# A third state tile, rows nine apart in HBM and filler matmuls in a four-layer network with a selective scan

## The chip, the cores and the metric

One core of one Trainium2 chip runs the whole program. The metric is the device time of one execution in microseconds (us). The kernel before takes 15384.8 us, the median of 3 runs (15377.52 to 15408.42).

## The reference, cut to what matters

The input x is (16, 192, 32, 32). Four layers follow each other, each in the form x = x + layer(group_norm(x)). Layer 0 is an mLSTM block with convolutions, layer 1 a channel attention with depthwise convolutions, layer 3 a roll-and-weight block with a 1x1 convolution. The change lies in layer 2, a selective scan over the 1024 pixels of an image in four directions (by rows, by columns, and both reversed), for 384 channels with 16 states each:

```python
D_INNER = 384
K = 4
N = 16
R = 12
...
        def step(h, xs_t):
            d_t, u_t, B_t, C_t = xs_t
            dA = jnp.exp(d_t[..., None] * A)
            h = h * dA + (d_t * u_t)[..., None] * B_t[:, :, None, :]
            y = jnp.einsum('bkdn,bkn->bkd', h, C_t)
            return (h, y)
...
    x_dbl = jnp.einsum('bkdl,kcd->bkcl', xs, x_proj_w)
    dts, Bs_, Cs_ = jnp.split(x_dbl, [R, R + N], axis=2)
    dts = jnp.einsum('bkrl,kdr->bkdl', dts, dt_w)
    delta = jax.nn.softplus(dts + dt_b[None, :, :, None])
    A = -jnp.exp(A_logs).reshape(K, D_INNER, N)
    ys = selective_scan(xs, delta, A, Bs_, Cs_, Ds.reshape(K, D_INNER))
```

## The kernel before, in words

**Stages.** `layer0` (L153) runs alone for about the first 3.1 ms. Then `LayersB` (L843) does layers 1 to 3: `prepare` (L1150) is layer 1 and the head of layer 2 of one image, `scans` (L1636) the scans of an image, `complete` (L1376) the end of layer 2 and layer 3. While the scans of image b run, `prepare` of image b+1 and `complete` of image b-1 are woven in between them as two background streams.

**The scans.** A unit of work is 16 channels with 8 states each, laid out as 128 partitions of 1024 pixels. Two units (`BLOCKS`) make a group of 16 channels with all 16 states, 24 groups a direction, 4 directions an image: 192 units, called slots, an image, and 3072 in all. For unit u of group n:

- `load_group` (L1811) loads the rows of delta (`dl`) and delta times u (`du`) of 16 channels from the HBM tensors `dld` and `dud`, each row repeated on 8 partitions: 16 rows of 4 KB read 8 times, 512 KB. `load_states` (L1807) loads the B and C rows (`bb`, `cb`) from `xdr` in the same way, 8 rows repeated 16 times, once a direction. The tiles `dl` and `du` have two buffers each.
- `decay` (L1851, ScalarE) makes dA = exp(dl times A); it is issued two slots ahead (`AHEAD`). `inputs_up` (L1845, ScalarE) copies `du` into one of two PSUM tiles `xt`, one group ahead.
- `inputs` (L1857, VectorE) multiplies `xt` by `bb`, both blocks of a group at the head of an even slot. `scan` (L1862, VectorE) then runs h = dA times h + xt along the pixels into `h[u % 2]`: two tiles of states, so that scan u can't start before the reader of scan u-2 is done.
- `outputs` (L1871, GpSimd) multiplies h by C into `hc`, one slot after the scan. `sums` (L1891, TensorE) adds the states up with a 0/1 matrix, four 32-row matmuls, one more slot later. `collect` (L1916, ScalarE) moves the accumulator out every fourth unit.

**The step sizes.** `front` (L1746) gives the pieces that make B, C, delta and delta times u of the next directions, at fixed slots of the 48 of a direction, counted from the direction's start (-24, -22, -18, -12, -6, 0, 6, 12 and a few after each). `ends` writes |x| into the tile `e` and relu(x) into `dlh`; `logs` turns `e` into log(1 + exp(-|x|)) in place; `park` adds `e` to `dlh` and multiplies by x into `duh`, both on GpSimd, and stores `dlh` and `duh` to HBM (L1794, L1795). Their matmuls use the PSUM bank "bf"; the two streams use "bp" and "bc".

**What sets the order.** The schedule is written by the program itself, with no reordering later (`manual_schedule`). `scans` keeps an estimated clock for each engine. A slot has an estimated length (`SLOT` = 4.83 us for an even one, 2.31 us for an odd one). In each slot it issues, in this order: inputs and scan, `outputs`, `sums`, `inputs_up`, `decay`, `collect`, the loads (`fetch`, L1820), the `front` pieces that are due, and then as many background pieces as the estimates (`Metered`, L782, `fits`, L1705) say will fit. An engine runs its instructions in that order, so a late instruction holds all that stands behind it. All loads and stores shown above are issued by SyncE's queue, in order as well. Near the end of an image, at slot 161 (`FETCH`), the head of the next image is completed and `fetch_xx` (L1372) loads its 1.5 MB `xx`, which `front` reads from slot 168 on, in the place of the current one.

Every operation of the background streams has the line L800 in the profile, since a helper (`Metered.issue`) records it.

Of the kernel before, what the change touches and what calls it, by code (L numbers as in the profile page):

```python
# [11 lines left out]
F32 = mybir.dt.float32  # L12
# [7 lines left out]
C, H, W = 192, 32, 32  # L20
L = H * W
# [752 lines left out]
ENGINES = ("PE", "ACT", "POOL", "DVE")  # L774
ALLOW = {"PE": 2.45, "DVE": 0.3}
OVER = {"PE": (0.8, 1.2), "ACT": (0.0, 1.5), "POOL": (0.5, 1.5)}
LEAST = {"PE": 1.0, "ACT": 0.6, "POOL": 0.8}
TABLE = 1.28
MARGIN = 0.6


# [61 lines left out]
class LayersB:  # L843
# [81 lines left out]
    def setup(self):  # L925

        tc, nc, cx, wp, I, NB = self.tc, self.nc, self.cx, self.wp, self.I, self.NB
        dp = self.dp
        self.dqd = dp.tile([6, 128, 9, 128], F32, name="dqd")
        self.dvd = dp.tile([2, 2, P6, 9, P6], F32, name="dvd")  # L930
        self.vd = dp.tile([P6, 2, L], F32, name="vd")
        self.x0d = dp.tile([P6, 2, L], F32, name="x0d")
        self.x2d = dp.tile([P6, 2, L], F32, name="x2d")
        self.xdr = dp.tile([K, 2 * N, L], F32, name="xdr")
        self.dld = dp.tile([K, 3, 128, L], F32, name="dld")
        self.dud = dp.tile([K, 3, 128, L], F32, name="dud")
        self.xxd = dp.tile([3, 128, L], F32, name="xxd")
        self.yd = dp.tile([3, 128, L], F32, name="yd")
        self.zd = dp.tile([NB, 3, 128, L], F32, name="zd")
        self.x1d = dp.tile([NB, P6, 2, L], F32, name="x1d")  # L940


        bn_g, bn_b = self.vec("bn_g", P6), self.vec("bn_b", P6)
        self.bsc = wp.tile([P6, 2], F32, name="bsc")
        self.bsh = wp.tile([P6, 2], F32, name="bsh")
        with tc.tile_pool(name="b_pre0", bufs=1) as pre:
            st = pre.tile([P6, 2, NB, 12], F32, name="st")
            for a in range(2):
                nc.scalar.dma_start(
                    st[:, a], self.sdram[:, a * P6 : (a + 1) * P6, :].rearrange("b p s -> p b s")  # L950
                )
            mv = pre.tile([P6, 2, 2], F32, name="mv")
            for a in range(2):
                nc.vector.bn_aggr(mv[:, a, :], st[:, a].rearrange("p b s -> p (b s)"))
            sd = pre.tile([P6, 2], F32, name="sd")
            nc.scalar.activation(sd, mv[:, :, 1], AF.Sqrt, bias=cx.eps5[0:P6])
            nc.vector.reciprocal(sd, sd)
            nc.vector.tensor_mul(self.bsc, sd, bn_g)
            nc.vector.tensor_mul(sd, mv[:, :, 0], self.bsc)
            nc.vector.tensor_sub(self.bsh, bn_b, sd)  # L960


        self.offb = wp.tile([P6, P6], F32, name="offb")
        nc.sync.dma_start(self.offb, I["c_off48"])
        self.temp = wp.tile([P6, 2], F32, name="temp")
        for a in range(2):
            for j in range(2):
                nc.sync.dma_start(
                    self.temp[48 * j : 48 * j + 48, a : a + 1],
                    I["temperature"][2 * a + j : 2 * a + j + 1].unsqueeze(0).to_broadcast([48, 1]),  # L970
                )

        self.dw2b = self.vec("dw_b", 128)
        self.pads = [wp.tile([128, H + 2, W + 2], F32, name="pad%d" % i) for i in range(2)]
        for t in self.pads:
            nc.gpsimd.memset(t, 0.0)

        self.xx = wp.tile([128, 3, L], F32, name="xx")
    def setup_scans(self):
# [52 lines left out]

        ring = lambda name, n, shape: [wp.tile(shape, F32, name=name + str(i)) for i in range(n)]
        self.y = wp.tile([128, 3, L], F32, name="y")
        self.dA, self.h, self.hc = ring("dA", 3, [128, L]), ring("h", 2, [128, L]), ring("hc", 3, [128, L])
        self.dl, self.du = ring("dl", 2, [128, L]), ring("du", 2, [128, L])
        self.bb, self.cb = ring("bb", BLOCKS, [128, L]), ring("cb", 3, [128, L])
        self.e, self.dlh, self.duh = (wp.tile([128, HL], F32, name=n) for n in ("e", "dlh", "duh"))
        self.xd = wp.tile([64 + XR, L], F32, name="xd")
        self.dtw = wp.tile([64 + R, INNER], F32, name="dtw")  # L1040
        self.xt = [self.xp.tile([128, L], F32, name="xt%d" % i) for i in range(2)]
# [108 lines left out]
    def prepare(self, b):  # L1150
# [67 lines left out]

        id6 = cx.ident[0:P6, 0:P6]
        at = sm.tile([P6, 2, P6], F32, tag="at", name="at", bufs=1)  # L1220
        kk = sm.tile([P6, 2, C], F32, tag="m1", name="kk", bufs=1)[:, :, 0:P6]
        rq = sm.tile([P6, 2], F32, tag="rq", name="rq")
        vs = [self.p4([P6, 2, HL], "vh") for _ in range(2)]
        for hf in range(2):
# [19 lines left out]
        for a in range(2):  # L1244
# [5 lines left out]
                nc, pk[:, ch(a)], [(qT[:, t, k0 : k0 + P6], qT[:, t, k0 : k0 + P6]) for t in range(NCH)]  # L1250
            )
        yield "DVE", 0
        nc.vector.tensor_mul(
            kk, pk.rearrange("p (a c) -> p a c", a=2), id6.unsqueeze(1).to_broadcast([P6, 2, P6])
        )
# [34 lines left out]
        yield "ACT", 0  # L1290
        for a in range(2):
            nc.scalar.mul(at[:, a, :], at[:, a, :], den[:, a : a + 1])
        m1 = sm.tile([P6, 2, C], F32, tag="m1", name="m1", bufs=1)
        m2 = sm.tile([P6, 2, C], F32, tag="m2", name="m2", bufs=1)
        for m_, w_ in ((m1, w1), (m2, wpf)):
            yield "PE", 0
            p = self.mm()[0:P6, 0 : 2 * C]
            for a in range(2):
                nc.tensor.matmul(p[:, a * C : (a + 1) * C], lhsT=at[:, a, :], rhs=w_[:, a, :], start=True, stop=True)
            yield "ACT", 0  # L1300
            nc.scalar.copy(m_, p.rearrange("p (a c) -> p a c", a=2))
        ds = [self.taps(P6, self.dvd[1, 0], I["dw_kv"][ch(0)], b == 0)]
        for hf in range(2):
            for a in range(2):
# [331 lines left out]
    def scans(self, b, more, carry):  # L1636
# [9 lines left out]
        for t in range(UNITS):  # L1646
            now = clock["DVE"]
            for e in ENGINES:
                clock[e] = max(clock[e], now)
            for s in (self.before, self.after):  # L1650
                while s.engine == "ACT" and not s.late and self.fits(s, now + SLOT[t % BLOCKS]):
                    self.advance(s)
            if t % BLOCKS == 0:
                for u in range(t, t + BLOCKS):
                    self.inputs(u)
            self.scan(t)
            clock["DVE"] += SLOT[t % BLOCKS]
            end = now + SLOT[t % BLOCKS]
            if t > 0 or carry:
                self.outputs((t - 1) % UNITS, t == 0)  # L1660
                clock["POOL"] += OWN["POOL"]
            if t > 1 or carry:
                self.sums((t - 2) % UNITS)
            if t % BLOCKS == BLOCKS - 1 and (more or t + 1 < UNITS):
                self.inputs_up((t + 1) % UNITS)
                clock["ACT"] += OWN["INPUTS"]
            if more or t + AHEAD < UNITS:
                self.decay((t + AHEAD) % UNITS)
                clock["ACT"] += OWN["DECAY"]
            if t > 1 or carry:  # L1670
                self.collect((t - 2) % UNITS)
            self.fetch(t, more, carry)
            self.bank = "bf"
            was = dict(self.spent)
            for piece in ahead.pop(t, ()):
                piece()
            for e in ENGINES:
                clock[e] += self.spent[e] - was[e]
            for e in ALLOW:
                have[e] = min(have[e], 0.0) + ALLOW[e] - self.spent[e] + was[e]  # L1680
            if more and t == FETCH:
                while self.parked < b + 2:
                    self.advance(self.after)
                self.fetch_xx()
            if t == UNITS - DIR_UNITS:
                while self.read < b:
                    self.advance(self.before)
            if t == 2:
                self.scanned = b
            streams = (self.before, self.after)[:: 1 if t % 2 else -1]  # L1690
            while any(self.fits(s, end) for s in streams):
                for s in streams:
                    if self.fits(s, end):
                        self.advance(s)
            self.slots += 1
        self.turns += K * more
        if not more:
# [4 lines left out]
                self.sums(u)  # L1702
            self.collect(UNITS - 1)

    def fits(self, s, end):  # L1705

        if not s.open(self.slots) or s.engine == "SP":
# [2 lines left out]
        if s.engine != "DVE":  # L1710
            end += OVER[s.engine][self.slots % BLOCKS]
        wait = s.inputs()
        if wait > at and (s.engine == "DVE" or wait + LEAST[s.engine] > end):
            return False
        return at < end + 0.1 and self.have.get(s.engine, 1.0) > 0.0

# [145 lines left out]
    def scan(self, u):  # L1862
        nc = self.nc
        n, blk = divmod(u, BLOCKS)
        k = n // GROUPS
        views = [self.h[u % 2], self.dA[u % 3], self.xt[(n + 1 + blk) % 2]]
        if k >= 2:
            views = [v[:, ::-1] for v in views]
        nc.vector.tensor_tensor_scan(*views, 0.0, op0=ALU.mult, op1=ALU.add)  # L1869

    def outputs(self, u, carried=False):  # L1871
# [1 line left out]
        n, blk = divmod(u, BLOCKS)  # L1873

        k = n // GROUPS - K * (carried and u == UNITS - 1)
        views = [self.hc[u % 3], self.h[u % 2], self.c_of(k, blk)]
        if n // GROUPS % 2:
            views = [views[0].rearrange("p (h w) -> p w h", w=W)] + [
                v.rearrange("p (w h) -> p w h", h=H) for v in views[1:]
# [147 lines left out]
```

## Time and profile before

| quantity | value |
|---|---|
| median of 3 runs | 15384.8 us |
| the profiled execution | 15416.19 us, of which the span from first to last instruction is 15414.4 us |
| busy over the span | PE 80%, DVE 80%, POOL 67%, ACT 59% |
| mean granted TensorE clock | 0.832 |
| scan stage, 3320 to 15250 us | 11930 us: DVE busy 10705.61, PE 9204.12, POOL 9503.52, ACT 7872.19; clock 0.80 |
| scan (DVE, L1869) | x3072, mean 2274 ns |
| input products (DVE, L1860) | x3072, mean 1227 ns |
| outputs (POOL, L1881) | x3072, mean 2371 ns |
| decay (ACT, L1853), copy of du (ACT, L1849) | 1146 ns each of 3072, 1014 ns each of 1536 |

How to read it: PE is TensorE, DVE VectorE, ACT ScalarE, POOL GpSimd, SP SyncE. A row of an engine gives its busy time and the idle time just before its instructions, with what ended that idle time ("<-"). The granted clock is the share of TensorE's full speed that its throttle let through. An fp32 matmul stands in the trace as two MATMUL records.

### The profile page before, as it was taken

How to read it: one execution, taken by the hardware profiler on the slowest of the kernel's cores; microseconds unless marked ns; L12 is line 12 of the kernel's file. 1: busy time of each engine (PE TensorE's matmuls, PEld its weight loads, DVE VectorE, ACT ScalarE, POOL GpSimd, SP SyncE). 2: the span in 40 equal slices, each digit the busy share in tenths (PEclk: the TensorE clock that was granted, in tenths of full speed). 3: DMA queues.
4: the chain of work that ended last, by engine and by line, in shares of the span. 5: the costliest groups of instructions: out<-in, count | busy, mean ns of one | idle time of the engine just before them, and what ended most of it. 6: DMA issues, size and time to landing. Idle time of an engine off the chain costs nothing.

```text
span 15414.4 us, 184312 instructions
## 1 busy us (share of the span) xinstructions
PE 12384.4 (80%) x65856; PEld 4810.3 (31%) x65856; DVE 12329.6 (80%) x10115; ACT 9160.4 (59%) x11881; POOL 10313.5 (67%) x6314
## 2 busy tenths in 40 slices
PE   8999999977777778777778787787878787878755
PEld 4444444422222222222222222222222222222212
DVE  4444444469988988888898989898988888889897
ACT  3333333345666666666666666666666666666665
POOL 2222222237787878787887878787878787878785
PEclk9999999978878887888888888887878787878766
DMA  1000000047878777878777777777777777777774
GB/s 30 15 15 15 17 15 15 14 126 185 214 181 212 185 207 182 208 180 210 189 203 191 199 195 198 195 198 194 197 196 194 195 197 199 194 200 186 200 182 129
DMA packets 884782, 2412.09 MB, mean 156 GB/s; under 512 B 146672, under 2 KB 266944, under 8 KB 876224
## 3 DMA queue, kind: packets, MB, share of 16 engines
q1 hardware_dynamic: 871168, 2397.50, 60.8%
q8 instruction: 532, 8.72, 0.2%
q10 hardware_dynamic: 12736, 3.04, 0.1%
q14 instruction: 346, 2.83, 0.1%
HBM read 2019.10 MB, written 364.30 MB: 155 GB/s over the span
## 4 chain that ended last, share of the span: by engine, by line
PE 19%; DVE 16%; POOL 14%; issue 13%; DMA 10%; ACT 7%; SPq 1%; DVEq 0%; POOLq 0%; ACTq 0%
PE mm L800 15%; DVE h L1869 10%; POOL hc L1881 9%; DVE xt L1860 5%; DMA dl<-dld 3%; PE acc L1911 3%; DMA du<-dud 2%; POOL t L800 2%; ACT dA L1853 2%; ACT xt L1849 2%; DMA y<-ydram 1%; DMA yh<-yd 1%; POOL dlh L800 1%; PE acc L1902 1%; DMA yd<-y 1%
## 5 line engine op out<-in xcount | busy, mean ns | idle before, releaser
L1881 POOL TENSOR_TENSOR hc<-h,cb 128x1024 f32<-128x1024 f32 x3072 | 7245.8, 2371 | 2087.6 <-DVE h L1869 1591.0
L1869 DVE TENSOR_TENSOR_SCAN h<-dA,xt 128x1024 f32<-128x1024 f32 x3072 | 6914.6, 2274 | 299.1 <-POOL hc L1881 292.0
L1860 DVE TENSOR_TENSOR xt<-xt,bb 128x1024 f32<-128x1024 f32 x3072 | 3633.2, 1227 | 904.0 <-ACT xt L1849 771.3
L1853 ACT ACTIVATE dA<-dl,A 128x1024 f32<-128x1024 f32 x3072 | 3507.3, 1146 | 810.3 <-DMA dl<-dld 703.4
L1911 PE MATMUL acc<-hc,sel 128*32 128x256 f32 x24576 | 2406.9, 473 | 1717.2 <-POOL hc L1881 1714.3
L800 PE MATMUL mm<-pad,dg 128*128 128x512 f32 (+1 forms) x5580 | 2911.4, 657 | 13.3 <-ACT pad L800 10.6
L1849 ACT COPY xt<-du 128x1024 f32<-128x1024 f32 x1536 | 1557.8, 1014 | 1350.9 <-DVE h L1869 1163.1
L627 POOL TENSOR_TENSOR D<-D,mask 128x256 f32<-128x256 f32 x768 | 542.7, 738 | 2101.1 <-DVE D L624 2101.1
L1911 PEld LDWEIGHTS acc<-hc,sel 128*32 128x32 f32 x24576 | 561.8, 120 | 4060.2 <-POOL hc L1881 2905.2
L800 PEld LDWEIGHTS mm<-pad,dg 128*128 128x128 f32 (+1 forms) x5580 | 999.1, 193 | 1491.8 <-issue 1370.3
L800 PE MATMUL mm<-x,wgt 96*128 96x512 f32 (+1 forms) x1664 | 1053.7, 769 | 146.8 <-ACT o L800 56.4
L1902 PE MATMUL acc<-y,ident 128*128 128x512 f32 x576 | 442.3, 859 | 447.3 <-ACT y L1921 445.9
L800 POOL TENSOR_TENSOR t<-x 96x768 f32<-96x768 f32 (+4 forms) x510 | 647.3, 1289 | 216.9 <-PE mm L800 216.8
L800 PE MATMUL mm<-d,xT 128*96 128x256 f32 x2048 | 567.9, 415 | 5.4 <-ACT o L800 5.0
L800 POOL TENSOR_TENSOR duh<-dlh,xx 128x512 f32<-128x512 f32 x384 | 537.6, 1400 | 30.1
L800 POOL TENSOR_TENSOR dlh<-dlh,e 128x512 f32<-128x512 f32 x384 | 488.5, 1272 | 103.0 <-ACT e L800 101.0
L800 PEld LDWEIGHTS mm<-x,wgt 96*128 96x128 f32 (+1 forms) x1664 | 339.3, 224 | 672.1 <-issue 363.5
L800 PE MATMUL mm<-xd,dtw 12*128 12x512 f32 x768 | 535.6, 783 | 10.3 <-ACT z L800 10.3
L391 PE MATMUL pc<-ypad,w_c 128*64 128x512 f32 (+1 forms) x1152 | 480.3, 664 | 74.2 <-PEq L751 41.5
L624 DVE SCALAR_TENSOR_TENSOR D<-D,s 128x256 f32<-128x256 f32 x768 | 272.0, 416 | 255.2 <-ACT D L620 255.2
L620 ACT ACTIVATE D<-s 128x256 f32<-128x256 f32 x768 | 233.4, 390 | 338.2 <-PE s L613 332.5
L800 PEld LDWEIGHTS mm<-d,xT 128*96 128x96 f32 x2048 | 328.0, 174 | 261.0 <-issue 164.0
(321 smaller groups left out, 14487.7 us busy)
## 6 DMA issues: line engine op xcount, KB each, us to landing
dl<-dld SPq DMA_DIRECT2D x1536, 512.0 KB
du<-dud SPq DMA_DIRECT2D x1536, 512.0 KB
dld<-dlh SPq DMA_DIRECT2D x384, 256.0 KB
dud<-duh SPq DMA_DIRECT2D x384, 256.0 KB
bb<-xdr SPq DMA_DIRECT2D x128, 512.0 KB
cb<-xdr SPq DMA_DIRECT2D x128, 512.0 KB
dg<-dqd SPq DMA_DIRECT2D x270, 192.0 KB
zd<-z SPq DMA_DIRECT2D x48, 512.0 KB
```

Source lines behind the costliest of these rows:

```text
L391: nc.tensor.matmul(p[r, :], lhsT=w_, rhs=v, start=(n == 0), stop=(n == 14))
L620: nc.scalar.activation(d, S[j][:, two], AF.Exp)
L624: nc.vector.scalar_tensor_tensor(d, d, 2.0, S[j][:, 2 * CH :], op0=ALU.min, op1=ALU.mult)
L627: nc.gpsimd.tensor_mul(d, d, mask)
L800: return f(out, *args, **kw)
L1849: self.nc.scalar.copy(self.xt[n], self.du[n])
L1853: self.nc.scalar.activation(self.dA[u % 3], self.dl[n % 2], AF.Exp, scale=self.A[:, blk, n : n + 1])
L1860: self.nc.vector.tensor_mul(self.xt[(n + 1 + blk) % 2], self.xt[n % 2], self.bb[blk])
L1869: nc.vector.tensor_tensor_scan(*views, 0.0, op0=ALU.mult, op1=ALU.add)
L1881: self.nc.gpsimd.tensor_mul(*views)
L1902: nc.tensor.matmul(acc, lhsT=self.cx.ident, rhs=self.y[:, g, half(pair)], start=True, stop=False)
L1911: nc.tensor.matmul(self.acc[rows4(q), q4(s)], lhsT=self.sel[:, m, :], rhs=self.hc[u % 3][:, q4(q)], start=False, stop=(s + m + blk == 3),)
```

## The change

- `h` becomes a ring of three tiles; `scan` and `outputs` index it with u % 3.
- To make room, the tile `e` is no longer a tile of its own but `duh`; `kk` of `prepare` takes a background slot "pa", and `m1` and `m2` take the two slots "w" of the weights.
- `xdr`, `dld` and `dud` are allocated with a further dimension of 9 (`PITCH`), of which only index 0 is used: a row of 4 KB lies 36 KB from the next one and no longer 4 KB.
- A new method `keep_busy` is called at the end of each slot. If TensorE's estimated clock lies more than 0.4 us (`IDLE`) before the slot's estimated end, it issues n matmuls of 128 by 256 (two MATMUL records each) whose result nobody reads, n being the room divided by 0.46 us (`FILL`), into the bank "bf", from `ident` and the first 256 columns of `xx`. It does nothing in the slots of `FRONT` and the two after each (23 of the 48 slots of a direction), and none in the last four slots of an image.
- `LEAST` becomes pairs with equal members, which changes no value.

```diff
+PITCH = 9
+FRONT = (-24, -22, -18, -12, -6, 0, 6, 12)
+IDLE, FILL = 0.4, 0.46
...
-        self.xdr = dp.tile([K, 2 * N, L], F32, name="xdr")
-        self.dld = dp.tile([K, 3, 128, L], F32, name="dld")
-        self.dud = dp.tile([K, 3, 128, L], F32, name="dud")
+        self.xdr = dp.tile([K, 2 * N, PITCH, L], F32, name="xdr")[:, :, 0, :]
+        self.dld = dp.tile([K, 3, 128, PITCH, L], F32, name="dld")[:, :, :, 0, :]
+        self.dud = dp.tile([K, 3, 128, PITCH, L], F32, name="dud")[:, :, :, 0, :]
...
-        self.dA, self.h, self.hc = ring("dA", 3, [128, L]), ring("h", 2, [128, L]), ring("hc", 3, [128, L])
+        self.dA, self.h, self.hc = ring("dA", 3, [128, L]), ring("h", 3, [128, L]), ring("hc", 3, [128, L])
...
-        self.e, self.dlh, self.duh = (wp.tile([128, HL], F32, name=n) for n in ("e", "dlh", "duh"))
+        self.dlh, self.duh = (wp.tile([128, HL], F32, name=n) for n in ("dlh", "duh"))
+        self.e = self.duh
...
-        kk = sm.tile([P6, 2, C], F32, tag="m1", name="kk", bufs=1)[:, :, 0:P6]
...
+        kk = self.slot("pa", [P6, 2, P6], "kk")
...
-        m1 = sm.tile([P6, 2, C], F32, tag="m1", name="m1", bufs=1)
-        m2 = sm.tile([P6, 2, C], F32, tag="m2", name="m2", bufs=1)
-        for m_, w_ in ((m1, w1), (m2, wpf)):
+        ms = []
+        for w_ in (w1, wpf):
...
+            m_ = self.slot("w", [P6, 2, C], "m", 2)
+            ms.append(m_)
...
+            self.keep_busy(t, end)
             self.slots += 1
...
+    def keep_busy(self, t, end):
+        at = t % DIR_UNITS
+
+        if any(0 <= (at - a) % DIR_UNITS <= 2 for a in FRONT) or t >= UNITS - 4:
+            return
+        n = int((end - self.clock["PE"] - IDLE) / FILL)
+        if n <= 0:
+            return
+        self.bank = "bf"
+        p = self.mm()
+        for i in range(n):
+            self.nc.tensor.matmul(
+                p[:, 0:256], lhsT=self.cx.ident, rhs=self.xx[:, 0, 0:256], start=True, stop=True
+            )
+        self.clock["PE"] += n * FILL
...
-        views = [self.h[u % 2], self.dA[u % 3], self.xt[(n + 1 + blk) % 2]]
+        views = [self.h[u % 3], self.dA[u % 3], self.xt[(n + 1 + blk) % 2]]
...
-        views = [self.hc[u % 3], self.h[u % 2], self.c_of(k, blk)]
+        views = [self.hc[u % 3], self.h[u % 3], self.c_of(k, blk)]
```

More of the change, by code (lines that the diff above doesn't have):

```diff
@@ L776 @@
 OVER = {"PE": (0.8, 1.2), "ACT": (0.0, 1.5), "POOL": (0.5, 1.5)}
-LEAST = {"PE": 1.0, "ACT": 0.6, "POOL": 0.8}
+LEAST = {"PE": (1.0, 1.0), "ACT": (0.6, 0.6), "POOL": (0.8, 0.8)}
 TABLE = 1.28
+PITCH = 9
+FRONT = (-24, -22, -18, -12, -6, 0, 6, 12)
+IDLE, FILL = 0.4, 0.46
 MARGIN = 0.6
@@ L1300, in prepare @@
             yield "ACT", 0
+            m_ = self.slot("w", [P6, 2, C], "m", 2)
+            ms.append(m_)
             nc.scalar.copy(m_, p.rearrange("p (a c) -> p a c", a=2))
+        m1, m2 = ms
         ds = [self.taps(P6, self.dvd[1, 0], I["dw_kv"][ch(0)], b == 0)]
@@ L1712, in fits @@
         wait = s.inputs()
-        if wait > at and (s.engine == "DVE" or wait + LEAST[s.engine] > end):
+        if wait > at and (s.engine == "DVE" or wait + LEAST[s.engine][self.slots % BLOCKS] > end):
             return False
```

## The prediction

> **What bounds the kernel now.** I read first the engines' busy time over the scan stage (the view of stretches, for 3320 to 15250 us; columns are length, then busy time of PE, PEld, DVE, ACT, POOL, then TensorE's clock, DMA share, GB/s).
>
> ```profile
> 3320.00:15250.00 11930.00, 9204.12 (x42460) 3210.49 (x42460) 10705.61 (x7115) 7872.19 (x9492) 9503.52 (x5234) 0.80 0.77 196
> ```
>
> VectorE is busy for 10,706 of 11,930 us, 90%: a floor, since the change takes no work from it. What can be won is its idle time, 11,930 - 10,706 = 1,224 us. So I asked next what VectorE waits for, and what ScalarE waits for, since it comes first there (3300 to 15000 us: total, times, longest).
>
> ```profile
> DVE xt L1860 <- ACT xt L1849: 766.9, 361, 30.0
> DVE h L1869 <- POOL hc L1881: 290.4, 231, 3.4
> DVE yh L800 <- PE mm L800: 40.7, 16, 5.0
> ...
> ACT dA L1853 <- DMA dl<-dld: 684.0, 237, 8.9
> ACT pad L800 <- PE mm L800: 345.9, 137, 6.4
> ACT xg L800 <- PE mm L800: 170.4, 75, 8.3
> ```
>
> The first row says that ScalarE's copy of du is late. It stands in ScalarE's queue behind evictions of the background streams, so I followed each of the 361 waits back to the last idle time of ScalarE before that copy. There it had waited for a TensorE matmul in about 540 us of the 767, for the load of `dl` in 110, for the store `zd` in 49, for `du` in 35. The same walk along GpSimd for the second row ends, for 173 of 297 us (the walk to the span's end counts 297), at `t` waiting for a matmul: its tile is free only when TensorE has read it. So some 750 us of VectorE's idle time begin at TensorE.
>
> The chain of waits over 3400 to 15250 us agrees; PE's shares are the largest:
>
> ```profile
> by line: PE mm L800 17.9%; issue 16.0%; DVE h L1869 12.7%; POOL hc L1881 11.9%; DVE xt L1860 6.2%; DMA dl<-dld 4.0%; PE acc L1911 3.7%; DMA du<-dud 3.1%; POOL t L800 3.1%; ACT dA L1853 2.8%; ACT xt L1849 2.7%; DMA y<-ydram 1.2%; DMA yh<-yd
> ```
>
> Why is TensorE late when it is only 77% busy? Two stretches of the same matmul (timeline: start, us, what):
>
> ```profile
> 8002.33 2.84 PE L800 MATMUL mm<-pad,dg 128*128 128x512 f32 x6
> ...
> 8010.45 3.78 PE L800 MATMUL mm<-pad,dg 128*128 128x512 f32 x4
> ```
>
> 0.47 us a record in one, 0.95 in the other: TensorE runs at full clock or at half. The planner's estimate for such a matmul (0.06 + 0.0017 x 512 = 0.93 us for two records) holds at full clock only.
>
> [...] its clock records hold only 1.0 and 0.5, in multiples of 3413 ns, and 40% of the scan stage is at 0.5 (0.6 x 1 + 0.4 x 0.5 = 0.80). Set beside TensorE's busy share in each window [...] of 591 half-clock windows under 80% busy none was followed by full clock, of 722 over 90% more than half were; of 279 full-clock windows under 40% busy none stayed full, of those over 60% at least 83%.
>
> [...] The trace has this: packets of 4 KB take 279 ns (median of 359 stretches with only `dl` and `du` moving), and 159 ns in the loads of `zd`[...]. In the view of stretches, last columns:
>
> ```profile
> 8028.00:8031.00 3.00, 1.89 (x13) 0.92 (x12) 3.00 (x2) 2.97 (x6) 2.29 (x2) 0.53 1.06 240
> 15268.00:15269.60 1.60, 0.45 (x8) 0.00 (x0) 1.60 (x3) 0.00 (x0) 1.60 (x1) 0.50 0.82 315
> ```
>
> 240 GB/s with all engines busy against 315 at 82%, that is 384.
>
> **The change part by part.**
>
> *Third h tile.* Scan u then waits for the output product of u-3, which has at least one odd slot (2.31 us planned) more; the waits average 290.4/231 = 1.26 us, 3.4 at most. So the 290 us go at that place. What is late next: in the list of VectorE's waits, 128 of these us are followed within 16 us by a wait for ScalarE, whose own cause (TensorE, DMA) isn't moved; there VectorE only arrives earlier and waits longer. 290 - 128 = 162: I take 165, with 60 and 290 as ends.
>
> *Filler matmuls.* Their number: I put each matmul record of the scans into its slot by order (a slot starts with the 8 records of L1911) and priced it as the planner does. The mean is 2.67 us a slot. Odd slots (2.31 us) have hardly any room; the even ones outside the blocked slots take 2.8 to 5.6 fillers, in all at most 2,680, since the planner's clock also counts waits. At full clock one costs two records of half the `pad` matmul's 512 columns, 2 x 0.47/2 = 0.47 us: 2,680 x 0.47 = 1,260 us of TensorE time, at the slot's end, where TensorE mostly waits next for `hc` (1,700 us, L1911 on L1881); that idle time is their cover. At half clock it is twice that and cover is gone in a late slot. The gain: they raise the busy share in 25 of 48 slots; half-clock time is as high in the blocked slots (0.51 to 0.57 in slots 0, 6, 8, and 0.72 in 30), where they do nothing. I estimate half clock falling from 40% to 28% of the stage. Lateness falls faster than that share, as short delays vanish wholly: I take 40% of the 540 + 41 us of waits that begin at TensorE: -230. Ends: -500 (clock near 1) and +0.
>
> *What fillers add by reading `xx`.* `fetch_xx` overwrites `xx`. Its load is issued at slot 162 of an image and lands 11.3 to 12.3 us later (15 images). The slot's own fillers (its planned load is 1.7 us, so about 5) read `xx`, so TensorE stands still until the load lands, about slot 165; behind it stand the sums, both streams' matmuls, then ScalarE's evictions and its copy of du. VectorE has some slack: I take 6 us of the 11.5, x 15 = +90. Ends: 0 and 170. SyncE in turn waits at that load for the fillers of slot 160: past by then, nothing.
>
> *Pitch.* If 4 KB packets fall from 279 to about 170 ns, a 512 KB load (8 packets an engine) falls from 2.2 to 1.4 us. A late `dl` is one that lands 7.7 us after its issue (median of the late ones, against 4.7 for all), as it stands behind other loads; with dl, du and bb some 60% of DMA time, about 2 to 2.5 us of that go, of a mean wait of 684/237 = 2.9. From VectorE's 110 + 35 + 49 and 16 us for `bb`, 210 in all, I take 55%: -115. [...] the ends are -210 and +40[...].
>
> *e in duh, kk, m1 and m2 in slots.* `ends` now also waits for the store of `duh`, issued last, with a landing of 5.5 us (median; 10.4 at the 95th percentile), three slots or some 12 us ahead. For `dlh`, stored one step earlier, the same wait came to 0.5 us in all. I take +10 (0 to 40). The load of `wx` now waits on SyncE for the last matmul with m1, with loads of `dl` queued behind: 15 x up to 3 us, mostly inside the 2 to 3 slots that a load has: +5 (0 to 45).
>
> Sum: -165 - 230 + 90 - 115 + 15 = -405. The profiled execution takes 15,416 us (its span 15,414), 31 over the median; I take the same -405 from the median 15,385: **14,980 us**, 2.6% less.
>
> **The rivals.** *Warm* (15%): TensorE stays at full clock nearly throughout, and `t`, evictions and copies come in time. Then -500 for the fillers, -250 for h, -150 for DMA, +90: -810, 14,575 us. [...] Against: blocked slots. *Moved* (21%): the wait for `hc` turns into one for ScalarE's copy, and the pitch changes nothing: -60 - 150 + 90 = -120, 15,265 us. For it: the two rows of waits stand close; against: 162 us have no such neighbour. *On the path* (9%), the other side: fillers run in slots that are late already, at a mean of both clocks, 0.70 us each: 1,880 us. PE has 2,806 of 11,930 us on the chain, 24%; with that share they cost 450, and with xx 170, 620; less 280 for h and pitch, +340: 15,725 us. Place: the end of even slots, in front of `sums`. It decides once more than 6% of filler time is on the path with no gain in clock ((280 - 170)/1,880), or 18% with the 230 us. Against it: TensorE's largest wait is right there. *Nothing* (4%): gains and stalls cancel.
>
> **How the numbers follow.** Main case 51%, -250 to -600. Warm 15%, Moved 21%, Nothing 4%, On the path 9%. A measurement here tells 0.2% (31 us) from no change. Faster: 51 + 15 + 20 = 86%; same: 4 + 1 = 5%; slower: 9%. The range runs from 14,600 (leaving out most of Warm, about 8%) to 15,300 (leaving out Nothing, On the path and no more).
>
> **What would show it.** DVE h on POOL hc from 290 to under 60 us. The clock in the scan stage from 0.80 to about 0.86, with 4,000 to 5,400 more MATMUL records. Stretches of `dl` and `du` alone at over 320 GB/s and a DMA share near 0.6; the late `dl` from 684 to about 300 us. A TensorE wait of about 9 us for xx<-xxd, 15 times. The forecast is wrong if the clock stays near 0.80, if the packets stay near 279 ns, or if DVE xt on ACT xt grows past 767 us.

## The result and the profile after

The changed kernel takes 15404.58 us (median of 20 runs, 15371.51 to 15420.25), the kernel before 15376.78 us in the same comparison: a ratio of 1.0016 with a 95% interval of 1.001 to 1.0022. It lies outside the range of 14,600 to 15,300 around the forecast of 14,980 us, and the sign was wrong too. The profiled execution's span is 15407.7 us. Lines have moved by 30 in the scans (the scan is now L1899, inputs L1890, decay L1883, copy of du L1879, outputs L1911, sums L1941); the helper of the background streams is L805, the fillers L1730.

The scan stage in the view of stretches (same columns as before: length, busy PE, PEld, DVE, ACT, POOL, clock, DMA share, GB/s):

```profile
3320.00:15250.00 11930.00, 9603.73 (x45310) 3729.36 (x45309) 10682.84 (x7122) 7872.99 (x9497) 9511.30 (x5238) 0.85 0.75 196
```

The clock went from 0.80 to 0.85, close to the forecast of 0.86, but with only 2,850 more MATMUL records (2,836 of them the fillers') where 4,000 to 5,400 were forecast. VectorE's busy time is what it was, so it idles as long as before. Its waits, and ScalarE's (3300 to 15000 us: total, times, longest), show what the idle time is made of now:

```profile
DVE xt L1890 <- ACT xt L1879: 1029.6, 373, 34.2
DVE h L1899 <- POOL hc L1911: 40.5, 39, 2.0
...
ACT dA L1883 <- DMA dl<-dld: 576.2, 209, 8.4
ACT z L805 <- PE mm L805: 361.1, 63, 16.2
ACT pad L805 <- PE mm L805: 275.5, 121, 7.8
```

The wait for `hc` has all but gone (290 to 40 us); the wait for ScalarE's copy of du has grown by as much (767 to 1,030), which the prediction had named as a sign of being wrong. From 3300 us to the end VectorE is idle for 1,331 us before and 1,358 after. The late `dl` fell by 108 us only, and ScalarE's `z` waits 241 us longer for a matmul (before: 119.7). TensorE's own waits give the reason for that last row:

```profile
PE acc L1941 <- POOL hc L1911: 1308.1, 844, 7.5
PE acc L1932 <- ACT y L1951: 267.1, 146, 4.7
PE mm L1730 <- DMA xx<-xxd: 223.8, 15, 15.6
```

The third row did not exist before: 15 times the fillers stand until the new `xx` has landed. The chain of waits (3400 to 15250 us) has it too, as two new members, `PE mm L1730` and `DMA xx<-xxd`, in place of what L805 gave up:

```profile
by line: issue 17.1%; PE mm L805 16.4%; DVE h L1899 13.8%; POOL hc L1911 11.4%; DVE xt L1890 7.3%; DMA dl<-dld 3.9%; PE acc L1941 3.8%; POOL t L805 3.1%; ACT xt L1879 2.5%; ACT dA L1883 2.0%; PE mm L1730 1.9%; DMA xx<-xxd 1.5%; PE acc L1932
```

One of the 15 stalls in the timelines of PE, SP and DVE (start, us, what, idle before it). The load leaves SyncE's queue at 3930.82; the fillers of a slot behind it stand on TensorE for 14.75 us, and VectorE then for 16.15:

```profile
3926.98 0.64 PE L1941 MATMUL acc<-hc,sel 128*32 128x256 f32 x8
3942.37 2.04 PE L1730 MATMUL mm<-xx,ident 128*128 128x256 f32 x4 [14.75 <-DMA xx<-xxd]
```

```profile
3930.82 0.53 SPq L1383 DMA_DIRECT2D xx<-xxd  x1
```

```profile
3937.26 4.45 DVE L1899 TENSOR_TENSOR_SCAN h<-dA,xt 128x1024 f32<-128x1024 f32 x2
3957.86 2.37 DVE L1890 TENSOR_TENSOR xt<-xt,bb 128x1024 f32<-128x1024 f32 x2 [16.15 <-ACT xt L1879]
```

### The profile page after: what moved, and what is told of

Its sections match the earlier page's. It is cut to its first block, busy times and chain, and to the rows that moved or that the text cites. A ratio compares the mean times of both kernels' runs of the same rounds, so it can differ in the third digit from the quotient of the medians.

```text
span 15407.7 us, 189554 instructions
## 1 busy us (share of the span) xinstructions
PE 12783.2 (83%) x68692; PEld 5329.9 (35%) x68692; DVE 12295.1 (80%) x10115; ACT 9156.4 (59%) x11881; POOL 10312.6 (67%) x6314
## 4 chain that ended last, share of the span: by engine, by line
PE 20%; DVE 18%; POOL 14%; issue 13%; DMA 8%; ACT 6%; SPq 1%; DVEq 0%; POOLq 0%; ACTq 0%
PE mm L805 14%; DVE h L1899 11%; POOL hc L1911 9%; DVE xt L1890 6%; DMA dl<-dld 3%; PE acc L1941 3%; POOL t L805 2%; ACT xt L1879 2%; ACT dA L1883 2%; PE mm L1730 1%; DMA xx<-xxd 1%; PE acc L1932 1%; POOL dlh L805 1%; DMA du<-dud 1%; DMA yh<-yd 1%
## 5 line engine op out<-in xcount | busy, mean ns | idle before, releaser
L1911 POOL TENSOR_TENSOR hc<-h,cb 128x1024 f32<-128x1024 f32 x3072 | 7243.1, 2372 | 2065.0 <-DVE h L1899 1456.1
L1899 DVE TENSOR_TENSOR_SCAN h<-dA,xt 128x1024 f32<-128x1024 f32 x3072 | 6889.3, 2270 | 40.5 <-POOL hc L1911 40.5
L1890 DVE TENSOR_TENSOR xt<-xt,bb 128x1024 f32<-128x1024 f32 x3072 | 3632.3, 1227 | 1163.0 <-ACT xt L1879 1033.6
L1883 ACT ACTIVATE dA<-dl,A 128x1024 f32<-128x1024 f32 x3072 | 3505.9, 1146 | 650.8 <-DMA dl<-dld 595.0
L1941 PE MATMUL acc<-hc,sel 128*32 128x256 f32 x24576 | 2241.4, 442 | 1375.9 <-POOL hc L1911 1373.4
L805 PE MATMUL mm<-pad,dg 128*128 128x512 f32 (+1 forms) x5580 | 2909.6, 657 | 13.2 <-ACT pad L805 11.0
L1879 ACT COPY xt<-du 128x1024 f32<-128x1024 f32 x1536 | 1557.3, 1014 | 1275.8 <-DVE h L1899 1094.6
L1941 PEld LDWEIGHTS acc<-hc,sel 128*32 128x32 f32 x24576 | 543.0, 116 | 3495.4 <-POOL hc L1911 2376.8
L805 PEld LDWEIGHTS mm<-pad,dg 128*128 128x128 f32 (+1 forms) x5580 | 995.5, 192 | 1476.1 <-issue 1360.9
L1730 PE MATMUL mm<-xx,ident 128*128 128x256 f32 x2836 | 917.3, 471 | 228.6 <-DMA xx<-xxd 223.8
L805 PE MATMUL mm<-x,wgt 96*128 96x512 f32 (+1 forms) x1664 | 992.5, 729 | 102.5 <-ACT o L805 51.3
L1730 PEld LDWEIGHTS mm<-xx,ident 128*128 128x128 f32 x2836 | 632.9, 236 | 549.3 <-issue 430.3
L805 POOL TENSOR_TENSOR t<-x 96x768 f32<-96x768 f32 (+4 forms) x510 | 647.7, 1291 | 252.4 <-PE mm L805 248.5
L805 POOL TENSOR_TENSOR dlh<-dlh,duh 128x512 f32<-128x512 f32 x384 | 488.6, 1272 | 115.7 <-ACT duh L805 115.7
L805 POOL TENSOR_TENSOR duh<-dlh,xx 128x512 f32<-128x512 f32 x384 | 538.1, 1401 | 30.1
L805 PE MATMUL mm<-d,xT 128*96 128x256 f32 x2048 | 546.9, 403 | 0.5 <-POOL d L805 0.5
L805 PEld LDWEIGHTS mm<-x,wgt 96*128 96x128 f32 (+1 forms) x1664 | 323.3, 213 | 593.1 <-issue 344.8
L805 PE MATMUL mm<-xd,dtw 12*128 12x512 f32 x768 | 491.5, 723 | 4.7 <-ACT z L805 4.7
```

The lines of the kernel that those rows point to most:

```text
L805: return f(out, *args, **kw)
L1730: self.nc.tensor.matmul(p[:, 0:256], lhsT=self.cx.ident, rhs=self.xx[:, 0, 0:256], start=True, stop=True)
L1879: self.nc.scalar.copy(self.xt[n], self.du[n])
L1883: self.nc.scalar.activation(self.dA[u % 3], self.dl[n % 2], AF.Exp, scale=self.A[:, blk, n : n + 1])
L1890: self.nc.vector.tensor_mul(self.xt[(n + 1 + blk) % 2], self.xt[n % 2], self.bb[blk])
L1911: self.nc.gpsimd.tensor_mul(*views)
```

## The experiments

Effects in us below are (ratio - 1) times 15,385, so that each run is taken against its own runs of the kernel before; 0.001 is 15 us. The changed kernel is +25.

### The parts, one at a time

The fillers read a constant tile in place of `xx` (a_perm), or are left out (b_nofill):

```diff
-                p[:, 0:256], lhsT=self.cx.ident, rhs=self.xx[:, 0, 0:256], start=True, stop=True
+                p[:, 0:256], lhsT=self.cx.ident, rhs=self.perm[:, 0:2].rearrange("p j h w -> p (j h w)"), start=True, stop=True
```

> The changed kernel, with the fillers reading a constant tile (perm) in the place of xx; number, shape and place of the fillers stay. Theory A (the fillers' read of xx eats what the rest gains): TensorE's 224 us of waiting for xx<-xxd go, slot 162 to 165 is short again, some 190 us are won: about 15,210 us. Theory B (the fillers delay TensorE's real work in general, xx is only one place of many): 15,330 or more.

> The changed kernel without the fillers (third h tile, aliases and pitch stay). Theory A: the h tile gains part of its 290 us, about 15,250 us, and TensorE's clock is back at 0.80. Theory C (the wait for hc only turns into one for ScalarE's copy of du, whatever the fillers do): 15,360 to 15,390, with DVE xt on ACT xt near 1,000 us.

Measured: a_perm 15313.79 us, ratio 0.9955 (0.9941 to 0.9968), -69; b_nofill 15339.1 us, 0.9973 (0.9963 to 0.9983), -42. So the read of `xx` costs 25 + 69 = 94 us, half of what theory A gave it, and fillers without it bring 69 - 42 = 27, give or take some 25. In a_perm ScalarE's `z` waits 108 us for a matmul, no longer than before the change (120). In b_nofill VectorE waits 933 us for the copy of du, which is nearer to theory C than to A.

The third tile with its aliases alone, without fillers and with rows 4 KB apart (c_h3: `PITCH = 1`, no `keep_busy`), and the pitch alone in the kernel before (d_pitch: the three allocations of the diff):

> Third h tile and the aliases alone: no fillers, rows 4 KB apart. If the pitch is worth nothing, as the unchanged 4 KB packets say (264 ns after, 269 before), this equals the run without fillers within 0.2%. If the pitch helps the late loads of dl, this one is 50 us or more slower than that.

> The kernel before with the rows 36 KB apart and nothing else. Pitch worth nothing: within 0.2% of before (15,377), 4 KB packets at 265 to 270 ns, late dl near 684 us. Pitch of use: 15,300 or less.

Measured: c_h3 15364.02 us, 0.9984 (0.9976 to 0.9993), -25; d_pitch 15362.7 us, 0.9987 (0.998 to 0.9993), -20. Together -45, against -42 for both in b_nofill: these two parts add up, and the whole is -42 - 27 + 94 = +25. The median 4 KB packet takes 265 ns in d_pitch, 269 in the kernel before. VectorE's waits in c_h3 (3300 to 15000 us):

```profile
DVE xt L1889 <- ACT xt L1878: 982.6, 408, 34.0
DVE h L1898 <- POOL hc L1910: 43.2, 38, 2.0
```

The exchange of 247 us of one wait for 216 of the other is thus the doing of the third tile and its aliases, with no filler in the kernel. Averaged by slot over images 1 to 14 it can be followed: slots 96 to 103 of an image become 2.73 us shorter, and slots 104 to 111 give 2.26 of them back. There the waits for `hc` at slots 103, 105 and 107 (8.3 us an image) become a wait for a matmul at 106 (2.5), for `hc` at 108 and 109 (2.7) and for `dl` at 111 (0.5 to 3.2).

The fillers of a_perm in the kernel before (j_fill):

> The kernel before with the fillers alone, reading the constant tile. If the parts add up, 25 us (as between the changed kernel without fillers and with fillers on the constant tile) less than before: 15,350 to 15,365. If fillers and the third h tile need each other: no difference, or more time than before, here.

Measured: 15381.81 us, 1.0002 (0.9994 to 1.0011), with a clock of 0.84 in the scan stage. Alone, in this number and these slots, the fillers bring nothing that can be measured.

### The loads of dl and du

Only the source of the loads changes, so that 128 different rows are read and none twice; the scans get wrong operands. g_distinct does it in c_h3, m_h2dist in the kernel before:

```diff
-                t, src[k, g, i * CW : (i + 1) * CW, :].unsqueeze(1).to_broadcast([CW, NBL, L])
+                t, src[k, g]
```

> The kernel with the third h tile alone (15,364 us), but each load of dl and du takes 128 different rows of the same tensor in the place of 16 rows 8 times each (so the scans work on wrong operands, with the same instructions and bytes). Theory F (reading the same row over and over is what slows the packets, and distance doesn't matter): 4 KB packets fall to 160 to 190 ns, the late dl by half or more, and the time shows what a pitch that works would have given: 60 to 115 us by the prediction's price. Theory G (it is the number of engines and other traffic at once): packets stay at 260 to 280 ns, time within 0.2%.

> The kernel before with loads of 128 different rows for dl and du (wrong operands for the scans, same instructions and bytes), two h tiles. With three h tiles the same loads gave 15,159. If the third tile's 290 us were swallowed by the late dl behind it, it is worth more once the loads are fast: this run 60 us or more above 15,159, 15,220 or more. If they are swallowed by TensorE-bound waits in the next slots: the third tile stays worth about 25 us here too, 15,170 to 15,200.

Measured: g_distinct 15158.9 us, 0.9858 (0.9838 to 0.9878), -218, that is 193 beyond c_h3; m_h2dist 15208.7 us, 0.9883 (0.9864 to 0.9902), -180. The third tile is worth 38 us between these two, beside 25 with slow loads: the intervals (about 30 us each way) are too wide to tell these apart. But the exchange of waits is there again. VectorE's waits in m_h2dist, then in g_distinct (3300 to 15000 us):

```profile
DVE xt L1860 <- ACT xt L1849: 611.3, 284, 30.3
DVE h L1869 <- POOL hc L1881: 240.0, 195, 3.3
```

```profile
DVE xt L1889 <- ACT xt L1878: 780.7, 357, 33.5
DVE h L1898 <- POOL hc L1910: 43.4, 41, 2.0
```

The third tile takes 197 us from one wait and 169 come back in the other. The prediction's walk (each wait for the copy of du followed back to ScalarE's last idle time) says what holds ScalarE. With slow loads, from before to c_h3, the load of `dl` goes from 109 to 245 us and TensorE from 564 (the prediction counted about 540) to 582. With fast loads, from m_h2dist to g_distinct, `dl` goes from 27 to 63 and TensorE from 540 to 624. So most of what comes back, 136 of 216 us, waits for `dl` while the loads are slow; once they are fast, half of it, 84 of 169, waits for TensorE.

The median 4 KB packet takes 159 ns in both runs. Two stretches with only `dl` and `du` moving, first of the changed kernel, then of g_distinct (last columns: DMA share, GB/s):

```profile
8033.50:8035.50 2.00, 1.78 (x16) 0.92 (x12) 2.00 (x2) 1.51 (x4) 1.37 (x1) 0.50 1.05 248
```

```profile
8033.00:8034.50 1.50, 1.39 (x4) 0.27 (x2) 1.50 (x1) 1.48 (x3) 1.50 (x3) 1.00 1.02 380
```

And g_distinct's scan stage and its late `dl`, for the same bytes a second in the stage:

```profile
3320.00:15100.00 11780.00, 9143.26 (x42708) 3187.45 (x42708) 10737.69 (x7198) 7904.69 (x9553) 9518.23 (x5242) 0.81 0.59 198
```

```profile
ACT dA L1882 <- DMA dl<-dld: 363.2, 162, 6.5
```

380 GB/s, a DMA share of 0.59 and a late `dl` of 363 us are close to what the prediction promised of the pitch (over 320, 0.6, 300). Reading distinct rows does it (159 ns a packet), and rows farther apart alone do not (265 ns in d_pitch).

Would fewer, longer rows do? k_pair lays a row of `dl` beside the row of `du` and fetches both in one load of 8 KB rows, still 8 times each (on the base of e_wide, below):

```diff
-        self.dld = dp.tile([K, 3, 128, PITCH, L], F32, name="dld")[:, :, :, 0, :]
-        self.dud = dp.tile([K, 3, 128, PITCH, L], F32, name="dud")[:, :, :, 0, :]
+        both = dp.tile([K, 3, 128, PITCH, 2, L], F32, name="dld")[:, :, :, 0]
...
-        for t, src in ((self.dl[n % 2], self.dld), (self.du[n % 2], self.dud)):
...
+        src = self.both[k, g, i * CW : (i + 1) * CW].unsqueeze(1)
+        self.nc.sync.dma_start(self.two[n % 2], src.to_broadcast([CW, NBL, 2, L]))
```

> The kernel with fillers in the third slots as well (15,282 us), with a channel's dl and du rows side by side in HBM, so that one load of 8 KB rows takes the place of the two loads of 4 KB rows: still 8 reads of the same row, but of twice the length, and half as many issues on SyncE. If what slows the packets is coming back at once to the same 4 KB: 8 KB packets near 318 to 380 ns (twice 159 to 190), late dl halved, 100 to 200 us faster, about 15,130. If reading a row repeatedly is slow whatever its length: packets near 540 ns, DMA share about 0.75 as before, 15,250 to 15,290.

Measured: 15535.14 us, 1.0097 (1.0079 to 1.0115). An 8 KB packet takes 594 ns (median), more than two of 4 KB (2 x 265 ns), and the first use of `dl` now waits for the whole 1 MB, which neither expectation had counted; against e_wide the run is 253 us slower (3300 to 15300 us):

```profile
ACT dA L1882 <- DMA dl<-dld: 1413.2, 537, 8.6
```

p_near is e_wide with `PITCH = 1`:

> The kernel with fillers in the third slots as well (15,282 us), rows 4 KB apart. If the pitch's small gain (25 us alone, 25 us beside the third h tile) is real and adds up: 15,295 to 15,320. If it was chance or is masked here: 15,270 to 15,290.

Measured: 15288.96 us, 0.994 (0.9927 to 0.9953), against e_wide's 0.9933: beside fillers the pitch's worth can't be told from nothing.

### How much is in TensorE's clock

e_wide is a_perm with the third slot of each blocked stretch given to fillers as well:

```diff
-        if any(0 <= (at - a) % DIR_UNITS <= 2 for a in FRONT) or t >= UNITS - 4:
+        if any(0 <= (at - a) % DIR_UNITS <= 1 for a in FRONT) or t >= UNITS - 4:
```

f_halfpad is a_perm with TensorE's work cut: seven of the nine taps of the 3x3 convolution take 256 of 512 columns, the planner's charge for them unchanged, so part of the convolution is left out:

```diff
-                    ps, lhsT=d[t // 3][:, t % 3, :],
-                    rhs=self.pads[i][0:p, 16 * hf + t // 3 : 16 * hf + t // 3 + 16, t % 3 : t % 3 + W],
+                n = 8 if 1 <= t <= 7 else 16
+                self.spent["PE"] += 0.0017 * W * (16 - n)
...
+                    ps[:, 0 : n * W], lhsT=d[t // 3][:, t % 3, :],
+                    rhs=self.pads[i][0:p, 16 * hf + t // 3 : 16 * hf + t // 3 + n, t % 3 : t % 3 + W],
```

> The kernel with fillers on the constant tile (15,314 us), and the fillers also allowed in the third slot of each blocked stretch, so in 7 more even slots of 48. Theory D (the fillers warm TensorE in slots where nobody waits for it; the waits stand in full slots): the clock rises by another 0.01 to 0.03 and the time stays within 0.2% (15,285 to 15,345). Theory E (clock is what counts, there were only too few fillers): 40 us or more faster, 15,270 or less. Theory B (fillers delay the real work): 15,350 or more.

> The kernel with fillers on the constant tile, with seven of the nine tap matmuls of the background streams' depthwise convolutions working on 256 of their 512 columns, the planner's estimates unchanged, so that order and places are the same (this leaves out part of the convolution's taps for half of each tile). TensorE's largest background group takes 39% less time. If TensorE's lateness in full slots is what ScalarE, and behind it VectorE, waits for: the waits for vf, v, pad, xg go and the time falls by 150 to 300 us, to about 15,100. If those waits only pass on to the next wait, as the wait for hc did: less than 60 us, 15,255 or more.

Measured: e_wide 15281.56 us, 0.9933 (0.9919 to 0.9946), -103, with 4,350 filler records and a scan-stage clock of 0.88; f_halfpad 15201.57 us, 0.9886 (0.987 to 0.9901), -175, that is 106 beyond a_perm, between what the two theories gave; e_wide lies between its theories too, next to D. The scan stage of a_perm, then of f_halfpad:

```profile
3320.00:15250.00 11930.00, 9704.32 (x45516) 3742.78 (x45520) 10736.93 (x7196) 7911.51 (x9541) 9520.67 (x5242) 0.84 0.75 196
```

```profile
3320.00:15100.00 11780.00, 9046.91 (x45314) 3844.44 (x45306) 10694.97 (x7144) 7867.32 (x9500) 9501.58 (x5235) 0.82 0.76 198
```

Some 650 us less of TensorE's busy time bring 106, a sixth. That is not the whole worth of TensorE's lateness: with less to do, TensorE also runs more at half clock (37% of the stage, 31% in a_perm; in the 8 us ahead of ScalarE's waits for it, 53% against 41%).

More fillers then: n_more simply fills to 0.8 us past the slot's end (`IDLE = -0.8`); q_free fills as far but charges the planner only for what e_wide would issue, so that the order of all other work stays:

```diff
-        n = int((end - self.clock["PE"] - IDLE) / FILL)
+        charged, n = (int((end - self.clock["PE"] - IDLE + m) / FILL) for m in (0, 1.2))
...
-        self.clock["PE"] += n * FILL
+        self.clock["PE"] += max(charged, 0) * FILL
```

> The kernel with fillers in the third slots as well (15,282 us), and each filled slot filled up to 0.8 us past its estimated end instead of 0.4 us before it, two or three fillers more a slot. Theory E (clock is what counts): clock above 0.90 and 20 us or more faster, 15,260 or less. Theory B (in a slot that is already late, a filler delays the sums and the streams' matmuls): 15,310 or more, and ScalarE waits longer for TensorE.

> The kernel with fillers in the third slots as well (15,282 us), again with each slot filled up to 0.8 us past its estimated end, but the added fillers not charged to the planner's clock, so that all other instructions keep their order (in the run that charged them the background pieces were pushed out of their slots: 17,408 us). Theory E (clock is what counts): clock above 0.90 in the scan stage, 20 us or more faster, 15,260 or less. Theory B (fillers in late slots delay the sums and the streams' matmuls): 15,310 or more, ScalarE waiting over 1,550 us for TensorE. In between: the two cancel.

Measured: n_more 17408.28 us, 1.1316 (1.1302 to 1.1331). This run says nothing of the clock's worth: the charged fillers left no room in the plan for the background pieces, which were then drained in one go (54 us more in slots 144 to 151 of each image, 118 more in slots 160 to 167). q_free 15120.96 us, 0.9837 (0.9821 to 0.9853), -251: faster than both kernels. This is what theory E gave. Its scan stage, then VectorE's waits (3300 to 15000 us):

```profile
3320.00:15050.00 11730.00, 10420.25 (x51986) 4756.52 (x51984) 10733.29 (x7194) 7911.31 (x9538) 9527.31 (x5242) 0.92 0.77 199
```

```profile
DVE xt L1890 <- ACT xt L1879: 775.7, 389, 33.7
...
DVE h L1899 <- POOL hc L1911: 28.3, 14, 2.0
```

Two last runs: r_full is q_free with 2.4 in the place of 1.2, and s_h2free has q_free's fillers in the kernel before, with two `h` tiles and near rows.

> The kernel with the uncharged fillers (15,121 us), each filled slot now filled up to 2.0 us past its estimated end. If the gain goes on with the clock: clock above 0.95 in the scan stage and 15,080 or less. If the fillers' own time in late slots now outweighs it (theory B, with a turning point): 15,160 or more.

> The kernel before (two h tiles, rows 4 KB apart) with the uncharged fillers of the 15,121 us run alone. If the clock is what counts by itself: 15,190 or less. If TensorE's gain reaches VectorE only when it may run ahead of GpSimd (third h tile): 15,250 or more.

Measured: r_full 15687.77 us, 1.0195 (1.018 to 1.021), +300; s_h2free 15212.56 us, 0.9886 (0.9871 to 0.9901), -175. r_full first, its scan stage and VectorE's waits (3300 to 15300 us); its clock is all but full and TensorE is busy for 95% of the stage:

```profile
3320.00:15600.00 12280.00, 11693.70 (x59846) 6138.80 (x59846) 10727.00 (x7167) 7904.03 (x9525) 9533.23 (x5242) 0.97 0.73 190
```

```profile
DVE xt L1890 <- ACT xt L1879: 1180.7, 514, 33.9
DVE gn_mg L805 <- PE mm L805: 76.1, 17, 7.7
```

Its fillers are busy for 4,179 us, q_free's for 2,432; of the 1,747 us between them 551 reach the end, 32%, net of what the higher clock gains. In s_h2free the waits are (3300 to 15300 us):

```profile
DVE xt L1882 <- ACT xt L1871: 613.5, 352, 30.3
DVE h L1891 <- POOL hc L1903: 235.6, 254, 3.6
```

s_h2free lies between its two expectations, nearer to the first: q_free's fillers bring 175 us by themselves, and both waits of VectorE's shrink. Third tile and pitch bring 76 more beside them (-251 in q_free), with intervals of about 25 us on either number; without fillers they bring 42, a difference that the intervals don't make sure.

## Why the prediction was wrong, by its steps

| step | forecast | measured |
|---|---|---|
| third h tile | -165 (60 to 290) | -25 (c_h3, with the aliases) |
| fillers | -230 (0 to -500) | 0 alone (j_fill), -27 beside the rest (a_perm less b_nofill) |
| fillers' read of `xx` | +90 (0 to 170) | +94 |
| pitch | -115 (-210 to +40) | -20 (d_pitch) |
| e in duh, m1 and m2 | +15 | not measured alone; in the changed kernel ScalarE waits 2 us for the store of `duh`, SyncE 4 us for the matmuls with `m` |
| sum | -405 | +25 |

Between -405 and +25 lie 430 us. The fillers' term is off by 200 to 230 of them, the third tile's by 140, the pitch's by 95; the read of `xx` came as forecast.

**Third tile.** The wait went as forecast, to 40 us. What failed is "290 - 128 = 162": that only the waits with a neighbour within 16 us would come back. c_h3 shows 216 of 247 us as longer waits for the copy of du. VectorE comes earlier to a place that ScalarE hadn't reached. By the walk above, ScalarE is held there mostly by `dl` (136 us of the 216), and with fast loads half by TensorE (84 of 169); the tile touches neither. A neighbour within 16 us was too short a view: both engines go through the same slots in order, and the time is given back wherever the other is next late, here within some 8 slots. The rival *Moved* had this right, with 60 us where 25 were measured, and the pitch too ("changes nothing"); its -150 for the fillers was wrong.

**Fillers.** The first half of the step came out: half clock was to fall from 40% to 28% of the stage, and in the trace of after it takes 31%, at a clock of 0.85. That is in part luck, for there are 1,418 fillers, about half of the 2,680 that the working allowed for. In the trace of after, too, the clock records hold only 1.0 and 0.5 (470 of each), in multiples of 3413 ns. What the prediction counted in the trace of before is much the same there: of some 350 half-clock windows of 3413 ns under 80% busy at most one was followed by full clock. The second half failed: "I take 40% of the 540 + 41 us of waits that begin at TensorE". Measured are 0 to 27 us. Two things are wrong in it.

*Place.* The table gives half clock as a share of the scan stage (3320 to 15100 us), and of the 8 us ahead of ScalarE's waits for TensorE, weighted by the length of these waits. The gain is against the same kernel without fillers (before or b_nofill).

| run | half clock, stage | half clock ahead of the waits | gain, us |
|---|---|---|---|
| before | 0.40 | 0.42 | |
| j_fill | 0.31 | 0.38 | 0 |
| a_perm | 0.31 | 0.41 | 27 |
| e_wide | 0.24 | 0.36 | 61 |
| q_free | 0.15 | 0.20 | 209 |
| s_h2free | 0.16 | 0.19 | 175 |

The fillers of the change go to slots with room in the plan; the full slots get none, and in the blocked ones they are forbidden. So the share ahead of the waits hardly falls. The gain follows the second column more nearly than the first, but both fall together, so no run separates place from number.

*Size.* In s_h2free half clock has fallen further than the prediction asked for, and yet of the 564 us of VectorE's wait for the copy that begin at TensorE, 402 are left. ScalarE's waits for TensorE fall only from 1,549 to 1,392 us (3300 us to the end), and the run by 175, net of what the fillers cost. TensorE is busy in 1,369 of the 1,392 us, with fillers in 62 of them. Most of what is left is thus the streams' own matmuls; that they are late by their place in the queue and their length is the likely reading, not a tested one, for a filler can also delay a matmul before the wait begins. *Warm*, at -500 for the clock, was nearly three times too high.

**The read of xx.** Right in mechanism; the size is right with some luck. A stall of 14.9 us on average (223.8/15) came where 9 were expected, and costs 94/15 = 6.3 us an image, where 6 were taken: more of the stall was absorbed than forecast. Reading another tile in the useless matmuls is worth more than the 27 us that they brought in a_perm.

**Pitch.** The wrong cause was removed. The loads of `zd`, at 159 ns, read each row once, and those of `dl` read it 8 times; the step took the distance between rows, which the diff changes, for the cause. That was the author's estimate, shown by no trace. d_pitch leaves the packets at 265 ns, g_distinct has 159 with the tensor's rows 4 KB apart. The term that hangs on the packets was, if anything, sized too small: with fast packets the loads are worth 180 us (two `h` tiles) to 193 (three), not 115. With two possible causes and no trace to choose between them, the term should have been weighed by the chance that spacing was the one.

**The rival On the path** didn't decide here, but exists: 32% of the filler time that r_full has beyond q_free's lands on the end, more than the 6% to 18% from which the rival would win. With 1,418 fillers, a_perm shows no such cost.

**Still open.** Why eight reads of one row are slow is not settled. Rows 36 KB apart (d_pitch) and rows of 8 KB (k_pair) don't help as long as each is read 8 times. g_distinct changes more than the repetition: a load then covers eight times as many different bytes, and how its rows fall to the engines is not shown. A fix (one read, then a copy on the chip) wasn't tried. In what measure number and place of the fillers count is open too.

## What to carry to other kernels

When two engines take turns in an order written out beforehand, the removal of one's wait is worth only what the other has to spare at the next places where it is late: 25 us of 247 here. Follow the wait some slots on before it is counted as gained, and expect the next cause to take over when one is removed.

Useless matmuls for TensorE's clock must read a tile that nothing rewrites (the read of `xx` cost 94 us here) and must not displace other work in the plan (n_more: 17408.28 us). They gained here as half clock fell just ahead of the waits (half clock there: 0.42 in the kernel before, 0.20 in q_free), and they had an optimum: beside the rest of the change, -251 us with 9,300 filler records, +300 with 17,294.

If a slow transfer has two possible causes, forecast with both, and weigh the gain by the chance that the change removes the right one.

## What was not expected of the hardware

- With loads that read each 4 KB row 8 times, the median 4 KB packet takes 265 to 269 ns whether the rows lie 36 or 4 KB apart, and 159 ns where all rows differ (248 against 380 GB/s while only these loads move); 8 KB rows read 8 times cost 594 ns.
- With useless matmuls, TensorE's clock can be brought to 0.92 (9,300 records) and 0.97 (17,294) of the scan stage; between these two each further us of filler costs 0.3 us of the kernel's time.
- Seven of nine convolution matmuls cut to half their columns went with a lower clock in the scan stage, 0.82 against 0.84 (f_halfpad, a_perm).
